# A fused attention and expert kernel: token blocks transposed by VectorE and put in place by transfers, half-height and half-width matmuls for the odd pieces, router and sort at other places

## The chip, the cores and the metric

One Trainium2 chip, one core. The time is device microseconds for one execution. Before the change: median 720.46 us of three runs (720.29 to 722.41). A core has TensorE (PE, matmuls and transposes), VectorE (DVE), ScalarE (ACT), GpSimd (POOL) and SyncE (SP, which here only issues transfers); each runs its own queue in order, and 16 DMA engines move the data.

## What is computed

All in float32. Two layers with a residual each:

- x (16 sequences of 100 tokens, 256 channels) is normalised, projected to queries of 16 heads of 64, and attends to a context of 361 rows of 192 channels (keys and values by projection, softmax, weighted sum). The result is projected back to 256 channels, with a bias, and added to x.
- The sum is normalised again (call it xn). A shared gated network of width 704, `silu(xn w1) * (xn w3)`, then `w2`, is computed for every token. A router of seven experts picks for each token the one of highest probability; that expert, a network of the same form, is computed for the token. Both are added to x with weights that come from the chosen probability.

## The kernel before

The 1600 tokens lie as 13 tiles of 128 (the last, tile 12, has 64 rows) in acc, and in four groups, tiles 0-2, 3-5, 6-8 and 9-12 (GROUPS, L41). xT holds normalised tokens with channels on the partitions, which is what matmuls that contract over channels read: first those of the first normalisation, for the queries, later those of the second, for router and shared network.

**Attention** is a loop over 32 steps s = (sequence b, half g of the heads) (L814), each some 15 us. In a step: scores of four pairs of heads (L645), their exponentials (ACT, L661), 32x32 block transposes on VectorE (L674), matmuls for later sequences put between (key_pairs and value_pairs, both by L568; queries L544), and in g = 0 the weighted sums of the sequence before (values, L717), whose operand aT was put together from the transposed blocks by 16 transfers of 32 partitions each (moved, L681 to L705; eight issued on SP, eight on POOL, L695), with over from row (L701) beside them. The PE order is written out by hand; in attention so are those of ACT, VectorE and SP; the other order follows the program. Scores and the products of L568 contract over 64 rows and run in two halves of the PE array; L717 writes 64 columns each, two side by side.

Small pieces of work are strung between by queues: norms (normalisation and router, one piece by part() behind each VectorE transpose and one at a step's end), turns (the PE transposes of a normalised group, taken at the start of a g = 0 step, L819) and fillers (projection and router, at the end of the scores of a g = 0 step, L856). When the last token of a group has been projected (project, L739), normalised(g, keep=True) strings in its second layer_norm (L166): moments, roots (with a power on POOL, L183), normalise (L188; the result goes to memory xn_d by SP, L197), and turn (L202): two PE transposes a tile by the identity (L208) and one ACT copy for two tiles (L211).

The context of one sequence has 361 = 2 x 128 + 105 rows. For two sequences, the guests (GUESTS, L50), the odd 105 rows travel in the padding of five other sequences' context, the hosts, and their values go by transfer (host, L582) to space in w2_sb.

**Shared network.** hidden (L408) makes for a group the 704 hidden rows: five whole chunks of 128 (L425) and a rest of 64 (HALF, L442), which lies in the upper 64 partitions of a sixth chunk whose lower part is zero. down (L454) contracts the six chunks for each tile (L460), adds the result to acc (L463) and sends it to base_d (SP, L466). Group 0 is done in the last step of attention and behind it, the others behind attention.

**Behind attention** (L936 to L954) the order on PE is: hidden of group 1, transposes of group 3, down of tile 3, router of group 3, down of tiles 4 and 5, the two matmuls of sort_tokens (L314), hidden of group 2, fill (L391, the token of each slot), hidden of group 3, down of groups 2 and 3. Between sort and the rest SP fetches the weights of the first four expert tiles (fetch, L901; 2.2 MB each); behind fill POOL gathers rows of xn_d (L919).

**Experts.** Tokens are sorted by expert in tiles of 128. A Switch (L1032) picks by their number one of seven straight programs of run (L995): eight products for the first part of a tile (L969, 16 matmuls), transposes of the next tile's tokens (turn, L957), three more, and the finish of the tile before (L977, L981), which goes out by POOL. The first turn(0) stands in front of the Switch (L1030).

Of the kernel before, what the change touches and what calls it, by code (L numbers as in the profile page):

```python
# [14 lines left out]
F32 = mybir.dt.float32  # L15
# [11 lines left out]
P = 128  # L27
# [12 lines left out]
HALF = I - NI * P  # L40
GROUPS = ((0, 1, 2), (3, 4, 5), (6, 7, 8), (9, 10, 11, 12))  # L41
FIRST, SECOND = (0, 1), (2, 3, 4, 5)
NS = (N - E) // P + E
NF = (N + P - 1) // P
WE = 2 * 2 * I + (NI + 1) * C
# [1 line left out]


FREE = P - JL
GUESTS = {6: (1, 2, 3, 4, 5), 13: (8, 9, 10, 11, 12)}  # L50
HOSTS = {host: (b, i) for b, hosts in GUESTS.items() for i, host in enumerate(hosts)}
HG = 8
WARM = 6
# [6 lines left out]
def xattn_moe(  # L60
# [66 lines left out]
        nc.tensor.matmul(nothing[:, :P], ones, ones, start=True, stop=True)  # L127

    nc.gpsimd.memset(acc[LAST:, NT - 1, :], 0.0)
    nc.gpsimd.memset(w2_sb[: P - HALF, NI, :], 0.0)  # L130

    def load_x(g):
        full = [t for t in g if t < NT - 1]
# [29 lines left out]

    biases = deque()

    def layer_norm(tiles, keep=False):  # L166


        n = len(tiles)
        of, xns = {}, []  # L170

        def moments(i):
            if i == 0:
                of["mv"] = small.tile([P, 4, 2], F32, name="mv")
                of["rstd"] = small.tile([P, 4], F32, name="rstd")
            st = small.tile([P, 6], F32, name="st")
            nc.vector.bn_stats(st, acc[:, tiles[i], :])
            nc.vector.bn_aggr(of["mv"][:, i, :], st)

        def roots():  # L180
            rstd = of["rstd"]
            nc.vector.tensor_scalar(rstd[:, :n], of["mv"][:, :n, 1], EPS, None, ALU.add)
            nc.gpsimd.tensor_tensor(rstd[:, :n], rstd[:, :n], power[:, :n], ALU.pow)  # L183

        def normalise(i):
            t = tiles[i]
            xn = small.tile([P, C], F32, name="xn", bufs=4)
            nc.vector.tensor_scalar(  # L188
                xn,
                acc[:, t, :],  # L190
                of["mv"][:, i, 0:1],
                of["rstd"][:, i : i + 1],
                ALU.subtract,
                ALU.mult,
            )
            if keep:
                nc.sync.dma_start(xn_d[t * P : t * P + rows(t), :], xn[: rows(t), :])  # L197
            else:
                biases.append(t)
            xns.append(xn)  # L200

        def turn():  # L202
            for i in range(0, n, 2):
                tr = bank()
                m = min(2, n - i)
                for o in range(m):
                    for k in range(2):
                        nc.tensor.transpose(  # L208
                            tr[:, ds((k * m + o) * P, P)], xns[i + o][:, ts(k, P)], ident
                        )  # L210
                nc.scalar.copy(  # L211
                    xT[:, :, ds(tiles[i] * P, m * P)],
                    tr[:, : 2 * m * P].rearrange("p (k n) -> p k n", k=2),
                )

        parts = [lambda i=i: moments(i) for i in range(n)] + [roots]
        return parts + [lambda i=i: normalise(i) for i in range(n)], turn

    def load_shared(i):

        if i < 4:
            k, o = i // 2, ds(i % 2 * I, I)
            nc.sync.dma_start(w13_sb[:, k, o], w13[ts(k, P), o])
        elif i == 4:
            nc.sync.dma_start(w2_sb[:, :3, :], w2[: 3 * P].rearrange("(i p) c -> p i c", p=P))
        else:
            r = w2[3 * P : NI * P].rearrange("(i p) c -> p i c", p=P)
            nc.sync.dma_start(w2_sb[:, 3:NI, :], r)
            nc.sync.dma_start(w2_sb[P - HALF :, NI, :], w2[NI * P :])

    def router(tiles):

# [175 lines left out]
    def hidden(g, hT, sp, width=NB, same_table=0):  # L408
# [1 line left out]

        n = sum(map(rows, g))

        nc.gpsimd.memset(hT[: P - HALF, NI, :n], 0.0)

        def product(to, at):
            for k in range(2):
# [25 lines left out]
        def rest():  # L442

            pa = bank()
            product(pa, NI * P)
            s = sp.tile([P, width], F32, name="s")
            nc.scalar.activation(s[P - HALF :, :n], pa[:HALF, :n], AF.Silu)
            nc.vector.tensor_tensor(
                hT[P - HALF :, NI, :n], pa[P - HALF :, :n], s[P - HALF :, :n], ALU.mult
            )  # L450

        return [lambda i=i: whole(i) for i in range(NI)] + [rest]

    def down(g, hT):  # L454

        for i, t in enumerate(g):
            r = rows(t)
            y = bank()
            for c in range(NI + 1):
                nc.tensor.matmul(  # L460
                    y[:r, :C], hT[:, c, ds(i * P, r)], w2_sb[:, c, :], start=(c == 0), stop=(c == NI)
                )
            nc.vector.scalar_tensor_tensor(  # L463
                acc[:r, t, :], y[:r, :C], coef[:r, t : t + 1], acc[:r, t, :], ALU.mult, ALU.add
            )
            nc.sync.dma_start(base_d[t * P : t * P + r, :], acc[:r, t, :])  # L466


    with ExitStack() as attn:
# [10 lines left out]
        def load_ctx(b, parts=1):  # L480
            cT = ap2.tile([P, NR, NJ * P], F32, name="cT")
            of = ctxT[b].rearrange("p (k n) -> p k n", k=NR)
            for i in range(parts):
                k = ts(i, NR // parts)
                nc.sync.dma_start(cT[:, k], of[:, k])
            return cT

        wq_r = wq.rearrange("p (u k m) -> p u k m", u=NU, k=2)
# [14 lines left out]
        def load_later(s):  # L503

            if 1 < s < 4:
                m = ts(s - 2, NCH // 2)
                nc.sync.dma_start(
                    wp_sb[:, m], wproj.rearrange("(m p) c -> p m c", p=P)[:, m]
                )
            if s == 3:  # L510
                nc.sync.dma_start(rb_sb, rbias.to_broadcast([P, E]))
                nc.sync.dma_start(rw_sb[:, :, :E], rwT.rearrange("(k p) e -> p k e", p=P))
            if s == 4 or s == 7:
                load_x(GROUPS[s // 3 + 1])
            if s == 6 or s == 9:
                normalised(GROUPS[s // 3])
            if 10 <= s < 14:
                load_shared(s - 10)
            if s in (2 * B - 3, 2 * B - 2):
                load_shared(s - 2 * B + 7)  # L520

        NA = 4
        ats, qT_bufs = [], []
# [215 lines left out]
        def project(t):  # L739
            r = rows(t)  # L740
            resT = resTs.pop(t)
            pp = bank()
            for c in range(NCH):
                nc.tensor.matmul(  # L744
                    pp[:r, :C], resT[:, c, QP : QP + r], wp_sb[:, c, :], start=(c == 0), stop=(c == NCH - 1)
# [5 lines left out]
        turns, fillers, norms = deque(), deque(), deque()  # L751

        def normalised(g, keep=False):
            parts, turn = layer_norm(g, keep)
            norms.extend(parts)


# [56 lines left out]
        for s, (b, g) in enumerate(steps):  # L814
# [1 line left out]


            if g == 0:
                while turns:  # L819
                    turns.popleft()()  # L820
                pairs = values_of.pop(b)
                if s == 0:
                    ask = lambda: qs.pop(0)() or (lambda: None)
# [18 lines left out]
            for i in range(n2):  # L842
# [7 lines left out]
                turning = then  # L850
                for _ in range(-(-len(pairs) // (n2 - i))):
                    product(pairs)
            if puts:
                puts.popleft()()
            if g == 0:
# [20 lines left out]
        while norms or fillers or turns:  # L876
# [2 lines left out]
                turns.popleft()()  # L879
            if fillers:  # L880
                fillers.popleft()()
        down(GROUPS[0][:2], hT0)
        for at in range(NG):
            values(B - 1, at, *held.pop(0))
        down(GROUPS[0][2:], hT0[:, :, 2 * P :])
        finished(B - 1)
        while fillers:
            fillers.popleft()()
# [36 lines left out]
            oob_is_err=False,  # L925
        )

    with tc.tile_pool(name="hs", bufs=1) as hs:
        def run_hidden(g):
            n = sum(map(rows, g))  # L930
            hT = hs.tile([P, NI + 1, n], F32, name=f"hT{n}")
            for piece in hidden(g, hT, sp):
                piece()
            return hT

        parts, turn_last = layer_norm(GROUPS[-1], keep=True)  # L936
        for one in parts:
            one()
        hT = run_hidden(GROUPS[1])
        turn_last()  # L940
        down(GROUPS[1][:1], hT)
        for one in router(GROUPS[-1]):
            one()
        down(GROUPS[1][1:], hT[:, :, P:])
        fill = sort_tokens(hs)
        for k in range(NW):
            fetch(k)
        hT2 = run_hidden(GROUPS[2])
        fill()
        for k in range(NX - 1):  # L950
            gather_into(xgs, xn_d, k)
        hT3 = run_hidden(GROUPS[3])
        down(GROUPS[2], hT2)
        down(GROUPS[3], hT3)  # L954
    hp = ctx.enter_context(tc.tile_pool(name="hp", bufs=2))

    def turn(k):  # L957
        tr = bank()
        for j in range(2):
# [1 line left out]
        xgT = xp.tile([P, 2, P], F32, name="xgT")  # L961
        nc.scalar.copy(xgT.rearrange("p k n -> p (k n)"), tr[:, : 2 * P])  # L962
        return xgT

    def products(to, xgT, w, units):

# [10 lines left out]
    def finish(k, hT, bg):  # L977
# [14 lines left out]
            oob_is_err=False,  # L992
        )

    def run(k, state, tiles):  # L995


        xgT, last = state
        w, hT = wexs[k % NW], hTs[k % 2]
        pa, pb, pc = bank(), bank(), bank()  # L1000
        n = (NI - 1) * P
        products(pa, xgT, w, [i * P for i in range(NI - 1)])
        products(pb, xgT, w, [I + HALF + i * P for i in range(NI - 1)])
        s = sp.tile([P, n], F32, name="sg")
        nc.scalar.activation(s, pa[:, :n], AF.Silu)
        nc.vector.tensor_tensor(
# [15 lines left out]
            gather_into(bgs, base_d, k + NX - 1)  # L1022
        if k and k + NW - 1 < tiles:
            fetch(k + NW - 1)
        return ahead, (k, hT, bgs[k % NX])

    n = nc.values_load(e_at[:, NS:], min_val=0, max_val=NS - NF)
    for k in range(NX - 1):
        gather_into(bgs, base_d, k)
    first = turn(0), None  # L1030

    for extra in tc.Switch(n, NS - NF + 1):  # L1032
        then = first
# [57 lines left out]
```

## Time and profile before

| what | value |
|---|---|
| median of the runs | 720.46 us |
| profiled execution, its own time | 722.64 us |
| its span, first to last instruction | 720.9 us |
| VectorE, ScalarE, GpSimd busy | 420.4, 280.5, 198.6 us |
| attention, to the last projection | up to 521.1 us |
| behind attention, to the first expert product | 521.1 to 598.5 us |
| experts, to the last matmul | 598.5 to 715 us |
| DMA engines' mean busy share, those two later stretches | 0.36, 0.68 |

How to read the lines of a profile: a group is line, engine, operation, result and operands with partitions x elements, count, then busy time, the mean length of one in ns, and the idle time ahead of it with what ended it. A line of waits is who waited for whom, microseconds in total, times, the longest. A timeline line is start, length, engine and line. An f32 matmul shows as two passes, so counts of matmuls are doubled; a transpose shows as one. A line of stretches has the stretch, its length, busy time of PE, PEld, VectorE, ScalarE and GpSimd with counts, granted PE clock, share of the DMA engines and GB/s.

### The profile page before, as it was taken

What the parts mean: (1) busy time and instruction counts of PE and PEld (TensorE: products, weight loads), DVE (VectorE), ACT (ScalarE), POOL (GpSimd) and SP (SyncE); (2) the same over time, 40 slices, a digit from 0 to 9 for tenths busy, and PEclk for the clock granted to TensorE, in tenths of its full rate; (3) what the DMA queues carried; (4) which work ended last, traced back from release to release, by engine and by line L of the source; (5) the groups of instructions that cost most, each with busy time, mean ns of one, the idle gap of its engine ahead of it and who ended that gap; (6) DMA issues with size and microseconds to landing.
All of it is one profiled execution on the core that took longest, in us unless ns stands there. A gap on an engine that the chain in (4) does not pass through costs nothing. (4 is left out here: it accounts for less than half of the span.)

```text
span 720.9 us, 14788 instructions
## 1 busy us (share of the span) xinstructions
PE 709.6 (98%) x5192; PEld 511.7 (71%) x5192; DVE 420.4 (58%) x1090; ACT 280.5 (39%) x791; POOL 198.6 (28%) x419
## 2 busy tenths in 40 slices
PE   9999999999999999999999999999999999999996
PEld 6557657667566766757667676656766588999996
DVE  2777866867787676776777768676247222122121
ACT  2564563534546354463644635543032101111110
POOL 4142322322432222422224222242010103343321
PEclk9999999999999999999999999999999999999999
DMA  7066656454484543636445454465004812898860
GB/s 263 21 143 156 163 143 162 93 144 125 115 214 114 155 118 87 169 89 177 103 113 160 111 146 111 115 160 130 30 30 177 355 37 64 313 347 335 309 248 23
DMA packets 54619, 109.38 MB, mean 152 GB/s; under 512 B 28665, under 2 KB 35964, under 8 KB 52612
## 3 DMA queue, kind: packets, MB, share of 16 engines
q1 hardware_dynamic: 43892, 81.94, 37.1%
q0 software_dynamic: 10352, 25.98, 13.7%
q8 instruction: 44, 0.72, 0.4%
q14 instruction: 43, 0.35, 0.2%
q10 hardware_dynamic: 288, 0.39, 0.2%
HBM read 60.96 MB, written 5.35 MB: 92 GB/s over the span
## 5 line engine op out<-in xcount | busy, mean ns | idle before, releaser
L661 ACT ACTIVATE at<-mm,nm 128x361 f32<-128x361 f32 x256 | 141.7, 559 | 171.4 <-DVE nm L658 171.2
L695 POOL DMA_DIRECT2D aT<-tb x256 | 126.1, 500 | 293.2 <-PE mm L717 100.2
L658 DVE TENSOR_REDUCE nm<-mm 128x1 f32<-128x361 f32 x256 | 123.4, 523 | 60.9 <-PE mm L645 60.0
L674 DVE STREAM_TRANSPOSE tb<-at 128x384 f32<-128x384 f32 x256 | 133.0, 558 | 4.5
L568 PE MATMUL mm<-cT,wk_sb 64*128 64x361 f32 x768 | 125.3, 465 | 1.2 <-DMA wk_sb<-in_wk 0.7
L568 PE MATMUL mm<-wv_sb,cT 64*128 64x512 f32 (+1 forms) x552 | 126.1, 589 | 0.0
L568 PEld LDWEIGHTS mm<-cT,wk_sb 64*128 64x128 f32 x768 | 74.8, 187 | 46.6 <-issue 4.2
L645 PE MATMUL mm<-kT,qT 64*128 64x361 f32 x512 | 97.2, 474 | 0.0
L568 PEld LDWEIGHTS mm<-wv_sb,cT 64*128 64x128 f32 (+1 forms) x552 | 53.2, 185 | 53.6 <-issue 43.4
L969 PE MATMUL mm<-xgT,wex 128*128 128x128 f32 x660 | 78.6, 275 | 0.7 <-ACT xgT L962 0.7
L969 PEld LDWEIGHTS mm<-xgT,wex 128*128 128x128 f32 x660 | 77.0, 192 | 1.8 <-issue 1.1
L717 PE MATMUL mm<-aT,v 128*64 128x100 f32 (+1 forms) x1472 | 72.5, 251 | 1.7 <-DMA over<-row 1.3
L645 PEld LDWEIGHTS mm<-kT,qT 64*128 64x128 f32 x512 | 47.7, 186 | 34.2 <-issue 8.8
L717 PEld LDWEIGHTS mm<-aT,v 128*64 128x64 f32 (+1 forms) x1472 | 67.2, 135 | 6.1 <-issue 3.4
L417 PE MATMUL mm<-xT,w_sb 128*128 128x384 f32 (+1 forms) x176 | 60.9, 503 | 0.0
L417 PEld LDWEIGHTS mm<-xT,w_sb 128*128 128x128 f32 x176 | 32.9, 190 | 26.1 <-issue 8.5
L661 ACT ACTIVATION_READ_ACCUMULATOR at<-mm,nm 128x1 f32 x256 | 50.4, 197 | 0.0
L744 PE MATMUL mm<-wp_sb,resT 128*128 128x256 f32 (+1 forms) x208 | 48.0, 384 | 0.0
L544 PE MATMUL mm<-xT,wq_sb 128*128 128x200 f32 x256 | 46.9, 336 | 0.0
L544 PEld LDWEIGHTS mm<-xT,wq_sb 128*128 128x128 f32 x256 | 43.4, 190 | 4.0 <-issue 1.5
L744 PEld LDWEIGHTS mm<-wp_sb,resT 128*128 128x128 f32 (+1 forms) x208 | 37.8, 186 | 11.2 <-issue 4.4
L608 ACT COPY kT<-mm 128x361 f32<-128x361 f32 x64 | 29.3, 460 | 39.5 <-PE mm L568 39.5
(143 smaller groups left out, 561.2 us busy)
## 6 DMA issues: line engine op xcount, KB each, us to landing
wex<-in_wex SPq DMA_DIRECT2D x15, 2176.0 KB
aT<-tb POOLq DMA_DIRECT2D x256, 80.2 KB, 3.1
aT<-tb SPq DMA_DIRECT2D x256, 80.2 KB
cT<-in_ctxT SPq DMA_DIRECT2D x15, 576.0 KB
over<-row SPq DMA_DIRECT2D x64, 100.0 KB
xn_d<-xn SPq DMA_DIRECT2D x12, 128.0 KB
base_d<-acc SPq DMA_DIRECT2D x12, 128.0 KB
w_sb<-in_w SPq DMA_DIRECT2D x4, 352.0 KB
```

Source lines behind the costliest of these rows:

```text
L417: nc.tensor.matmul(to[:, :n], w13_sb[:, k, ds(at, P)], xT[:, k, ds(g[0] * P, n)], start=(k == 0), stop=(k == 1),)
L544: nc.tensor.matmul(pq[:, o, :], wq_sb[:, u, k, ts(o, P)], xT[:, k, ts(g, QG * LQ)], start=(k == 0), stop=(k == 1),)
L568: nc.tensor.matmul(to[o][:height, :width], *operands(o, k), start=(k == 0), stop=(k == NR - 1),)
L608: nc.scalar.copy(kT[:, c, :], to[0][:, :LKV])
L645: nc.tensor.matmul(sc[o][:, :LKV], qTs[b // QG][r, c, ts(b % QG, QB), :], kTs[b][c // 4][r, c % 4, :], start=True, stop=True,)
L658: nc.vector.tensor_reduce(nm[:, o : o + 1], sc[o][:, :LKV], AX.X, ALU.max, negate=True)
L661: nc.scalar.activation(at[:, o, :LKV], sc[o][:, :LKV], AF.Exp, bias=nm[:, o : o + 1], accum_out=sums[:, o : o + 1],)
L674: nc.vector.transpose(tb[:, :, :, o, i * QR : i * QR + 32].rearrange("p j k n -> p k j n"), at[:, o, :].rearrange("p (k j n) -> p k j n", ...
L695: queue.dma_start(aT[ts(j, 32), i].rearrange("p k o n -> p (k o n)"), tb[ts(i, 32), j].rearrange("p k o n -> p (k o n)"),)
L717: nc.tensor.matmul(av[ts(o, DK), i, :], v[:n, ds((2 * c + o) * DK, DK)], aT[:n, :, j, o, ts(i, QR)], start=(j == 0), stop=(j == NJ - 1),)
L744: nc.tensor.matmul(pp[:r, :C], resT[:, c, QP : QP + r], wp_sb[:, c, :], start=(c == 0), stop=(c == NCH - 1))
L969: nc.tensor.matmul(to[:, ts(o, P)], w[:, ds(j * 2 * I + u, P)], xgT[:, j, :], start=(j == 0), stop=(j == 1),)
```

## The change

1. **Blocks.** Second normalisations (keep) are no longer transposed by PE. normalise transposes each tile in 32x32 blocks on VectorE into a scratch (the second half of w13_sb in attention, a tile of its own behind it), and move(k) puts the blocks in place in xT with 16 transfers for each half k of the channels, eight issued on SP and eight on POOL, each 32 partitions by the group's tiles by 32 elements (128 bytes). turn does nothing for them, so ACT's copies go as well. The moves are two more pieces in norms; they fall in steps s = 14, 20 and 28, behind the second or third scores or at the end.
2. **Place of loads.** As the scratch lies in w13_sb, its second half is loaded at s = 28 and w2 at s = 29 (before: at 12 and 13, and 29 and 30). Guest 6 becomes guest 7, its hosts 2 to 6. Context that hosts nobody is loaded without padding. The remaining PE transposes (turns) come behind the first scores and products of a step.
3. **Pairs.** For five pairs of tiles the rests of 64 lie in different halves of the partitions (LOWER), and their last, half-height matmuls follow one another at the end of both tiles' sums. w2's rest is loaded into both halves.
4. **Two halves.** For tile 12, in project and down, the chunks are summed in two halves of 64 columns side by side; ACT copies the second half and VectorE adds both.
5. **Order behind attention.** hidden of group 1, down of 3, 5 and 4, router of group 3, three pieces of hidden of group 2, sort, the rest of group 2, two pieces of group 3, fill and gathers, the rest of group 3, down of 6 and 7, 12, 9 and 10, turn(0), down of 8 and 11, the first 16 products of expert tile 0, then the Switch.

The PE order by the two programs differs, apart from moved turns and guests, in these counts: 52 PE transposes of xn become 26; everything else is split or moved.

```
+PAIRS = ((0, 1), (5, 4), (6, 7), (9, 10), (8, 11))
+LOWER = tuple(b for _, b in PAIRS)
-GUESTS = {6: (1, 2, 3, 4, 5), 13: (8, 9, 10, 11, 12)}
+GUESTS = {7: (2, 3, 4, 5, 6), 13: (8, 9, 10, 11, 12)}
...
             if keep:
                 nc.sync.dma_start(xn_d[t * P : t * P + rows(t), :], xn[: rows(t), :])
+                nc.vector.transpose(xb[:, :, ts(i, 32)], xn.rearrange("p (c n) -> p c n", n=32))
...
+        def move(k):
+            for q in range(4):
+                for c in range(4):
+                    queue = nc.gpsimd if (q + c) % 2 else nc.sync
+                    m = n if q * 32 < LAST else full
+                    to = xT[ts(c, 32), k, ds(tiles[0] * P, m * P)]
+                    of = xb[ts(q, 32), 4 * k + c, : m * 32].rearrange("p (i n) -> p i n", n=32)
+                    queue.dma_start(to.rearrange("p (i n) -> p i n", n=P)[:, :, ts(q, 32)], of)
...
+    def two_halves(y, products):
+        n = len(products) // 2
+        for i in range(n):
+            for o in range(2):
+                nc.tensor.matmul(
+                    y[ts(o, LAST), :C], *products[o * n + i], start=(i == 0), stop=(i == n - 1)
+                )
+        high = bp_sb[:LAST]
+        nc.scalar.copy(high, y[LAST:, :C])
+        return high
...
+        if len(tiles) == 2:
+            for (t, hT, i), y in zip(tiles, ys):
+                r = slice(0, HALF) if t in LOWER else slice(P - HALF, P)
+                nc.tensor.matmul(
+                    y[:, :C], hT[r, NI, ts(i, P)], w2_sb[r, NI, :], start=False, stop=True
+                )
...
+        blocks = hs.tile([P, 8 * P], F32, name="blocks")
+        parts, turn_last = layer_norm(GROUPS[-1], blocks)
+        for one in parts:
+            one()
+        hT = run_hidden(GROUPS[1])
+        down([(3, hT, 0)])
+        down([(5, hT, 2), (4, hT, 1)])
+        for one in router(GROUPS[-1]):
+            one()
+        hT2, pieces = run_hidden(GROUPS[2], 3)
+        fill = sort_tokens(hs)
+        for k in range(NW):
+            fetch(k)
+        for piece in pieces:
+            piece()
+        hT3, pieces = run_hidden(GROUPS[3], 2)
+        fill()
+        for k in range(NX - 1):
+            gather_into(xgs, xn_d, k)
+        for piece in pieces:
+            piece()
+        down([(6, hT2, 0), (7, hT2, 1)])
+        down([(12, hT3, 3)])
+        down([(9, hT3, 0), (10, hT3, 1)])
+        ahead = turn(0)
+        down([(8, hT2, 2), (11, hT3, 2)])
...
-    first = turn(0), None
+    first = ahead, None, first_products(0, ahead)
```

## Prediction

> **What bounds the kernel now.** I read the page first (busy shares and slices), then the waits of TensorE (PE), then PE's timeline around the change, and last the groups of the operations that are added or removed.
>
> ```profile
> PE 709.6 (98%) x5192; PEld 511.7 (71%) x5192; DVE 420.4 (58%) x1090; ACT 280.5 (39%) x791; POOL 198.6 (28%) x419
> PE   9999999999999999999999999999999999999996
> ```
>
> PE is busy in every slice but the last. A busy PE need not be at its peak, so I ask whether it ever waits:
>
> ```profile
> PE mm L717 <- DMA over<-row: 1.3, 1, 1.3
> PE mm L127 <- DVE ones L124: 1.1, 1, 1.1
> PE mm L969 <- ACT xgT L962: 0.7, 1, 0.7
> ```
>
> These are its three longest waits; with the small ones they come to some 6 us of 720.9. So a PE instruction that goes away is worth its own length, anywhere, and any new wait of PE costs its full length. The timeline gives the steps (start, length, group):
>
> ```profile
> 513.97 7.21 PE L744 MATMUL mm<-wp_sb,resT 128*128 128x256 f32 x32
> 521.12 14.46 PE L417 MATMUL mm<-xT,w_sb 128*128 128x384 f32 x44
> 535.41 1.04 PE L208 MATMUL mm<-ident,xn 128*128 128x128 f32 x8
> 536.28 2.76 PE L460 MATMUL mm<-w_sb,hT 128*128 128x256 f32 x12
> 538.97 0.64 PE L240 MATMUL mm<-xT,rw_sb 128*32 128x128 f32 x16
> ...
> 597.33 0.44 PE L960 MATMUL mm<-ident,xg 128*128 128x128 f32 x2
> 598.50 3.81 PE L969 MATMUL mm<-xgT,wex 128*128 128x128 f32 x32 [0.74 <-ACT xgT L962]
> ```
>
> Each f32 matmul is two passes (12 for six matmuls), and a full pass of 256 columns takes 0.22 us. The router's matmuls of the last group (L240) stand 18 us behind the end of the projections (521.12).
>
> **Part 1, PE work removed.** The groups by form:
>
> ```profile
> L568 PE MATMUL mm<-cT,wk_sb 64*128 64x361 f32 x768 | 125.3, 465 | 1.2 <-DMA wk_sb<-in_wk 0.7 <-DMA cT<-in_ctxT 0.5
> L208 PE MATMUL mm<-ident,xn 128*128 128x128 f32 x52 | 7.6, 281 | 0.6 <-DVE xn L188 0.6
> L744 PE MATMUL mm<-wp_sb,resT 128*64 128x256 f32 x16 | 3.7, 382 | 0.0
> L460 PE MATMUL mm<-w_sb,hT 128*64 128x256 f32 x12 | 2.8, 383 | 0.0
> ```
>
> Transposes: 26 of the 52 at L208 go, three sets of 6 in attention (0.78 us each in the timeline) and the 8 at 535.41 (1.04): 3.4 us.
>
> Last tile in two halves: L568 shows what two half arrays side by side bring: 163 ns a pass (125.3/768) where 361 columns on the full array would be 361 x 0.857 = 309 (14.46/44/384 = 0.857 ns a column). The 16 passes of L744 then take about 8.5 steps of 0.22 and the 12 of L460 about 6.5: 1.9 and 1.4 us in place of 3.7 and 2.8, less 0.1 each for the change of mode: 3.0 saved, say 2.9. The 64-column pairs of L717 do worse (67 ns against 86 for 100 columns); by that ratio it would be 1.4. I take 2.9, since 256 columns are longer than a weight load of 64 columns (137 ns), which 100 are not.
>
> Pairs: in five pairs two full chunks (4 passes, 0.88 us) become two half-height ones. Alone, the second pass of the first runs beside the first of the second: three steps, 0.66 us. Here a rule speaks against the change: the Trainium skill (TensorEngine Tiling (Array Packing), Tiling Modes, Key Properties) says that a change of tiling mode drains TensorE. The timeline agrees: a score pair (L645) right behind the column-split L717 takes 0.71 us from start to start, one between half-height products 0.61, so some 0.1. Without the drain five pairs save 1.1 us; with one drain each (the way back I count as hidden) 0.6; with two, nothing. I take 0.7, range 0 to 1.8.
>
> Idle: turn(0) moves in front of the last pair (4.4 us and more of PE), which hides the 0.74 us wait: 0.7. Sum removed: 3.4 + 2.9 + 0.7 + 0.7 = 7.7 us.
>
> **Part 2, what is added on PE.** The branch (Switch) now stands behind 16 products of the first expert tile and in front of its other six. Before, it lay in the gap from 597.33 to 598.50. So it costs 0 (PE's queue covers it) to 1.1; I take 0.5. ScalarE, VectorE and the DMA queues branch earlier than they need.
>
> **Part 3, the blocks in attention (groups 0 to 2).** Per group: three VectorE transposes of 128x256, 0.39 us each as an estimate (L674: 558 ns for 384 columns); ScalarE loses two copies of 0.6; 32 DMAs, 16 on SP and 16 on POOL, of 128-byte runs, 96 or 128 runs each. VectorE is 58% busy and PE waits for it nowhere; I cost these at nothing. The DMAs stand in steps with g = 0, behind the moved() of the step before and in front of their own step's. SP needs about 16 x 0.6 = 10 us (the two issues of over at 307.52, with 256 runs each, took 1.30 together). What queues behind is row, aT and over of that step, which PE reads two steps (some 30 us) later. POOL has the same place and 8 aT (4 us) behind it: 16 x t + 4 us in 30. Free up to t = 1.6 us an issue, and the router reads these blocks two steps later. The late loads of w13 (s = 28) wait for the moves on SP and have two steps before their first reader. The shift of the guest by one batch changes no count of matmuls. Cost 0; if cover failed, each of three groups would stop PE at L717.
>
> **Part 4, the blocks in front of the experts.** Here the cover is thin. After the change the projections end 2.3 + 0.1 + 1.7 earlier, T = 517.0. The normalisation chain took 5.8 us before (521.12 to 526.90). It grows by a ScalarE copy and a second add (0.75) and four transposes (1.6): moves can start at T + 8.1 = 525.1. PE reaches the router after hidden (14.3 us from start to start) and the three downs (16 chunks at 0.44 and a pair, 7.8): T + 22.1 = 539.1. So 14.0 us are there for 16 issues on POOL and the landing of the last:
>
> ```profile
> L695 POOL DMA_DIRECT2D aT<-tb x256 | 126.1, 500 | 293.2 <-PE mm L717 100.2 <-PE mm L208 41.1 <-DVE nm L658 39.7
> L919 POOL DMA_INDIRECT xg<-xn_d,slot_token x15 | 15.2, 1015 | 25.3 <-DMA wex<-in_wex 17.7 <-PE mm L969 2.5 <-DMA aT<-tb 2.2
> ```
>
> A POOL issue with 32 runs takes 0.50 us, an indirect one with 128 rows 1.0. Landing is 3.1 us in the median (DMA issues of the page). The new one is direct like the first and has as many runs as the second. With t = 0.5: 8.0 + 3.1 = 11.1, no wait. With t = 1.0: 19.1, a wait of 5.1. I take t = 0.8: 15.9, a wait of 1.9. The rule against it: the Trainium skill (DMA: Bandwidth & Descriptors, Anatomy of one DMA) fits a POOL-issued DMA as 2.0 us plus bytes/436e3. 16 KB one after another would be 16 x 2.04 = 33 us, a wait of 19 to 22. But eight aT issues of 80 KB each pass in 3.9 us here, so fixed parts overlap, and the row goes before the fit. The DMA engines themselves:
>
> ```profile
> 308.00:311.00 3.00, 3.00 (x18) 1.39 (x16) 2.32 (x6) 2.02 (x6) 0.00 (x0) 1.00 0.49 108
> ```
>
> In this stretch mostly the 512 runs of over move: 0.49 x 3 us x 16 engines / 512 = 46 ns a run at most. 3584 runs on 16 engines are 10.3 us, within the 14. SP issues (10 us) land in time too.
>
> Behind the router: its VectorE chain took 5.7 us (538.97 to 544.7) and now has 7.9 (three pieces of hidden). Sort to fill: 9 us of VectorE (545.5 to 554.5) against some 13 of PE. The four expert weights had landed at 573.7 (DMA shares in stretches of 2 us), 29 us behind the sort's matmuls; now some 43 pass until first_products. The gathers have 22 us before turn(0). All at nothing.
>
> **Sum.** -7.7 + 0.5 + 1.9 = -5.3 us: the span goes from 720.9 to 715.6. The profiled execution took 722.64, 2.2 more than the median 720.46 and 1.7 more than its span; the same difference from the median gives 715.2.
>
> **Rivals.** (A) The cover holds, t at or below 0.65: -7.2 and the pairs between 0.7 and their best, 711.9 to 713.9, middle 713. For it: POOL's aT issues hardly vary. (B) The likeliest, t of 0.65 to 1.05: a wait of 0 to 6, 713.9 to 718.3. (C) Half arrays don't overlap when they stand alone (ratio of L717, pairs nothing: removed 5.5) and the wait is 4 or more: 719.5, within the noise. For it: L717's ratio; against: L568's. (D) Slower: POOL's issue of strided short runs. Break-even is 16t + 3.1 - 14.0 = 7.2, t = 1.13 us. At the skill's 2.04 the wait is 21.7 and the time 720.46 - 7.2 + 21.7 = 735, and beyond t = 1.6 the aT transfers in attention would be late as well. For it: no run of before shows 96 or 128 short runs from POOL; against: both rows above are below 1.13.
>
> **Numbers.** A 0.33, B 0.38, C 0.17, D 0.12. Range 711.8 to 720.2, which leaves D and the ends out. 0.3% (2.2 us) is about what a measurement of this kernel can tell from no change: faster (below 718.3) 0.72, same 0.16, slower 0.12.
>
> **What would show it.** Right: L208 at 26 passes; PE busy lower by about 7 us; a PE wait at L240 for a DMA xT, 0 to 5 us, as the only new one; POOL's xT issues at 0.6 to 1.0 us. Wrong: PE waits at L717 for aT or over in steps with moves, xT issues above 1.1 us, a gap of over 1 us behind the 16 first products, or the half passes at L460 and L744 at 0.2 us each.

## The result and the profile after

The median of seven runs is 727.13 us (724.04 to 729.97), beside 720.71 us for the kernel before (seven runs, 720.29 to 722.75): 1.0079 times as long, with a 95% interval of 1.0061 to 1.0096. The forecast was 715.2, faster; it is slower. The profiled execution took 725.76 us with a span of 723.9.

The page of the changed kernel, busy times and slices (a digit is a tenth of the slice):

```profile
PE 707.0 (98%) x5166; PEld 511.1 (71%) x5166; DVE 425.6 (59%) x1113; ACT 276.9 (38%) x785; POOL 232.0 (32%) x481
PE   9999999999998999999999999989999998999996
```

26 matmul records fewer, as foreseen, but PE's busy time fell by only 2.6 us where 7.0 were expected, and three slices are no longer full. Idle time (span less busy) rose from 11.3 to 16.9 us. The longest waits of TensorE in the changed kernel (sum, times, longest):

```profile
PE mm L781 <- DMA over<-row: 3.1, 1, 3.1
PE mm L709 <- ACT at L725: 2.7, 1, 2.7
PE mm L1001 <- DVE hgT L1091: 2.0, 1, 2.0
```

The second and third have no like in the list of before. The first has (L717 there, 1.3 us), but at another place, 204.86 in the timeline of before. The one new wait that was forecast, the router's (L265 here, L240 before), is not there. Each of the three happens once; PE's timeline (start, length, group, and in brackets the idle time just before) places them:

```profile
224.30 0.88 PE L709 MATMUL mm<-kT,qT 64*128 64x361 f32 x4
227.84 1.89 PE L709 MATMUL mm<-kT,qT 64*128 64x361 f32 x8 [2.65 <-ACT at L725]
...
481.18 3.38 PE L781 MATMUL mm<-aT,v 128*64 128x100 f32 x48 [3.12 <-DMA over<-row]
...
603.73 0.41 PE L1001 MATMUL mm<-ident,xg 128*128 128x128 f32 x2 [1.98 <-DVE hgT L1091]
603.97 6.71 PE L1048 MATMUL mm<-xgT,wex 128*128 128x128 f32 x44
```

I call them W1 (attention step s = 14), W2 (the weighted sums at the end of s = 30) and W3 (behind the 16 products that now stand in front of the Switch). The name of a releaser is inferred, and W2's is misleading: L781 reads aT and v, while over is read by VectorE (L796). In e2 below the same wait is put down to aT, and in e4 PE goes on at 474.84, only 0.4 us after the last issue of over had ended. So I read W2 as a wait for the aT that SP issues just ahead of over.

The lengths hold a second loss. The 44 passes at 603.97 take 6.71 us; before, the same 44 took 5.08:

```profile
602.37 5.08 PE L969 MATMUL mm<-xgT,wex 128*128 128x128 f32 x44
```

The stretches of after (length, PE busy, granted clock, DMA share, GB/s) say why, here those behind W1:

```profile
228.00:230.00 2.00, 2.00 (x9) 0.91 0.82 195
230.00:232.00 2.00, 2.00 (x6) 0.50 0.86 254
232.00:234.00 2.00, 2.00 (x8) 0.74 0.65 187
```

Read each row's clock as a mixture of 1.0 and 0.5: 0.36 + 2.0 + 1.04 = 3.4 us at half the clock, which costs 1.7 us of work. The same happens behind W2 (482.2 to 485.6) and W3 (605.1 to 608.5). The kernel before shows no such drop until its last 5 us.

This gives an account of the profiled execution. PE's work went down by 7.8 us (709.6 to 701.8, the busy time of the kernel e12 below, which does the changed work without a drop), the three drops add 5.2 (the rest of the busy time, 707.0 less 701.8; three times the 1.7 read from the clock would be 5.1), idle time adds 5.6: 3.0 in all, from 720.9 to 723.9. The medians lie further apart (6.4 us), since the profiled execution of before was 1.9 above its median (722.64) and that of after 1.4 below. The other executions of after have mean clocks of 0.986 (729.97 us) to 0.993 (724.04 us), those of before mostly 0.998 to 0.999. A drop of 3.4 us lowers the mean by 3.4 x 0.5 / 724 = 0.0023, so that by this estimate they hold two to five each; the profiled one held three. Five is more than W1 to W3 account for, and where the others fall no trace shows.

### The profile page after: what moved, and what is told of

Same layout as the page of the kernel before. It is cut to its first block, busy times and chain, and to the rows that moved or that the text cites. A ratio compares the mean times of both kernels' runs of the same rounds, so it can differ in the third digit from the quotient of the medians.

```text
span 723.9 us, 14995 instructions
## 1 busy us (share of the span) xinstructions
PE 707.0 (98%) x5166; PEld 511.1 (71%) x5166; DVE 425.6 (59%) x1113; ACT 276.9 (38%) x785; POOL 232.0 (32%) x481
## 5 line engine op out<-in xcount | busy, mean ns | idle before, releaser
L1048 PEld LDWEIGHTS mm<-xgT,wex 128*128 128x128 f32 x660 | 78.6, 195 | 1.0 <-issue 0.3
L781 PE MATMUL mm<-aT,v 128*64 128x100 f32 (+1 forms) x1472 | 73.6, 253 | 3.5 <-DMA over<-row 3.1
L781 PEld LDWEIGHTS mm<-aT,v 128*64 128x64 f32 (+1 forms) x1472 | 68.1, 136 | 8.0 <-ACT pr L291 3.3
L813 PE MATMUL mm<-wp_sb,resT 128*128 128x256 f32 x192 | 46.1, 395 | 0.0
L813 PEld LDWEIGHTS mm<-wp_sb,resT 128*128 128x128 f32 x192 | 36.9, 196 | 10.1 <-issue 2.5
```

The lines of the kernel that those rows point to most:

```text
L781: nc.tensor.matmul(av[ts(o, DK), i, :], v[:n, ds((2 * c + o) * DK, DK)], aT[:n, :, j, o, ts(i, QR)], start=(j == 0), stop=(j == NJ - 1),)
L813: nc.tensor.matmul(pp[:r, :C], resT[:, c, QP : QP + r], wp_sb[:, c, :], start=(c == 0), stop=(c == NCH - 1))
L1048: nc.tensor.matmul(to[:, ts(o, P)], w[:, ds(j * 2 * I + u, P)], xgT[:, j, :], start=(j == 0), stop=(j == 1),)
```

## The experiments

The theory behind the first four: three separate places, each with its own cause (the turns' new place, the loads of the shared weights behind the moves on SP, the products in front of the Switch), each a wait and a drop of the clock. The rival: the blocks' transfers disturb attention in general, or the drops come from PE's load as a whole, so that undoing one place moves the loss elsewhere. All ran in three rounds. Ratios are to the kernel before on the same chip.

| kernel | median us (range) | ratio [95%] |
|---|---|---|
| e1: after, Switch first | 723.75 (720.83 to 726.46) | 1.0038 [1.0021, 1.0056] |
| e2: after, turns first | 722.31 (720.14 to 724.74) | 1.0031 [1.0014, 1.0048] |
| e3: after, loads at s = 29 | 720.70 (718.50 to 722.34) | 0.9995 [0.9982, 1.0008] |
| e4: all three | 714.94 (714.92 to 716.02) | 0.9927 [0.9910, 0.9943] |
| e5: before, products ahead of the Switch | 722.74 (721.61 to 725.31) | 1.0027 [1.0016, 1.0038] |
| e6: before, turns behind the first products | 724.73 (723.78 to 725.26) | 1.0049 [1.0032, 1.0065] |
| e7: after, W1 filled | 724.58 (721.79 to 727.14) | 1.0063 [1.0038, 1.0087] |
| e8: after again | 726.39 (724.54 to 728.40) | 1.0085 [1.0065, 1.0105] |
| e9: e4 without blocks | 716.83 (715.97 to 717.98) | 0.9949 [0.9932, 0.9966] |
| e10: e4 without pairs | 716.14 (714.35 to 716.78) | 0.9930 [0.9913, 0.9946] |
| e11: e9 with the loads at s = 28 | 716.46 (716.23 to 716.66) | 0.9943 [0.9926, 0.9959] |
| e12: e4 again | 715.33 (715.09 to 716.87) | 0.9934 [0.9917, 0.9950] |

**e1, the Switch before the products.**

```
-    first = ahead, None, first_products(0, ahead)
+    first = ahead, None, None
```

> The changed kernel, with the 16 first products of expert tile 0 behind the Switch again; turn(0) stays where the change put it. Theory (each of three new TensorE waits costs its own length and then some 1.7 us of halved clock; the third, 1.98 us at 603.7, is the Switch standing between products and transposes): the wait and the clock drop at 604 to 608 go, 3.7 us below the changed kernel, about 723.4 in the median; the other two waits stay. Rival 1 (the halved clock comes from denser TensorE work and not from waits): the wait goes, 2 us, and the drop comes at another place, 725.1. Rival 2 (the wait is for a PSUM bank that VectorE frees, as the trace labels it): nothing changes, 727.

3.4 us less than after. W3 and its drop are gone; what stands there is a shorter wait for the bank of the last down. PE's timeline of e1:

```profile
600.06 3.81 PE L1048 MATMUL mm<-xgT,wex 128*128 128x128 f32 x32 [1.22 <-DVE acc L525]
```

W1 (2.65) and W2 (4.03) stay, each with its drop.

**e2, the turns at the start of the step, as before.**

```
             if g == 0:
+                while turns:
+                    turns.popleft()()
...
-                while g == i == 0 and turns:
-                    turns.popleft()()
```

> The changed kernel, with the remaining TensorE transposes at the start of a g = 0 step again. Theory (VectorE's normalise of group 0 has no free xn buffer until the transposes of group 3 have run; behind the first scores and products they run one product later, so VectorE stands 3.3 us and TensorE runs out of PSUM banks): the wait of 2.65 us at 227.8 and its clock drop go, 4.3 us below the changed kernel, about 722.8. Rival (VectorE is late by the three added block transposes of 0.45 us in that step): the wait stays at 1.5 us or more, gain below 2 us.

4.8 us less. W1 is gone without a remainder, although the block transposes that the rival blames are still there; W2 (3.43, with a drop) and W3 (1.71, without) stay.

**e3, the second half of w13 loaded one step later.**

```
-            if s in (2 * B - 4, 2 * B - 3):
-                for i in range(2):
-                    load_shared(2 * (s - 2 * B + 5) + i)
+            if s == 2 * B - 3:
+                for i in range(2, 6):
+                    load_shared(i)
```

> The changed kernel, with the second half of w13 loaded at s = 29 behind that step's transfers and not at s = 28. Theory (at s = 28 SP issues 16 moves in 11.4 us and then the two loads, so row, aT and over of s = 29 leave some 3 us later): over of s = 29 leaves about 2.5 us earlier, the wait of 3.1 us at L781 falls to about 1 and brings no clock drop, 4 us below the changed kernel, about 723. Rival (the moves alone make SP late; the loads of 0.9 us are nothing): the wait falls by 1 us to about 2.2, with a clock drop still, 726.

6.4 us less, more than W2 and its drop explain. W2 shrinks to 0.40 us ahead of the sums and 0.88 in their middle, and brings no drop; but in the profiled execution W1 (2.65) brought none either, and W3 (1.91) did. How many drops an execution takes varies, and that W2's absence lowers their number elsewhere is not shown.

**e4, all three.**

> All three edits together (first products behind the Switch, transposes at the start of the step, w13 at s = 29). Theory: the costs add, 3.7 + 4.3 + 4 = 12 us below the changed kernel: span about 712, median 713 to 715, clock 0.998 or more, no TensorE wait above 1.5 us. Rival (the waits hide one another, or another wait takes their place): above 718.

714.94, 5.8 us faster than before and 12.2 below after's 727.13. The single gains, against the same 727.13 (3.4, 4.8, 6.4), sum to 14.6; against e8, after's second measurement, each is 0.7 less, and they sum to 12.4 against 11.5. Page and waits of e4:

```profile
PE 701.3 (98%) x5166; PEld 506.6 (71%) x5166; DVE 425.2 (60%) x1113; ACT 277.4 (39%) x785; POOL 232.1 (33%) x481
```

```profile
PE mm L632 <- DMA cT<-in_ctxT: 1.3, 2, 0.7
PE mm L132 <- DVE ones L129: 1.1, 1, 1.1
PE mm L781 <- DMA aT<-tb: 1.1, 1, 1.1
PE mm L1048 <- DVE acc L525: 1.0, 1, 1.0
```

No wait above 1.1 us, no drop of the clock before the last 5 us, and PE's work is 8.3 us below that of before. The rival falls: undone together, the three places leave little behind. What stays of W2 is the third line (the moves are still there), of W3 the fourth (a bank of the last down, as in e1).

**e5 and e6, one part alone on the kernel before.** e5 takes the 16 products out of run and puts them in front of the Switch; e6 takes the turns behind the first scores and products.

```
...
-    first = turn(0), None
+    ahead = turn(0)
+    first = ahead, None, first_products(0, ahead)
```

> The kernel before, with one part alone: the 16 first products of expert tile 0 in front of the Switch. Theory (the Switch takes TensorE's sequencer some 2 us, hidden before in the wait for xgT and in the queue ahead of it): a wait of some 2 us in front of the second transposes and a clock drop behind it, 3.7 above before, 724.4. Rival (the wait in the changed kernel comes from its own bank order): no wait, 720.7.

```
             if g == 0:
-                while turns:
-                    turns.popleft()()
...
+                while g == i == 0 and turns:
+                    turns.popleft()()
```

> The kernel before, with one part alone: TensorE transposes behind the first scores and products of a step (guests, blocks and loads as before). Theory a (place of the transposes alone): VectorE stands some 3 us in step 14, TensorE waits 2 us or more with a clock drop, 724.5 or more. Theory b (it needs the guest's missing value product as well: here step 14 has one product more to run meanwhile): wait below 1 us, no drop, within 1 us of 720.7.

PE's timeline of e5, where only the Switch's place is changed:

```profile
603.73 0.41 PE L960 MATMUL mm<-ident,xg 128*128 128x128 f32 x2 [2.20 <-issue]
```

The gap is the Switch's own: PE waited for nothing the profile shows ("issue"), and the VectorE operation named at W3 in after had ended 0.7 us before PE went on (1.4 in e5), so it was only the last thing to have happened. Here the gap brought no drop in the profiled execution, and the price is 1.8 us, not the 3.7 of a gap with one. PE's timeline of e6:

```profile
229.68 3.08 PE L645 MATMUL mm<-kT,qT 64*128 64x361 f32 x8 [1.75 <-ACT at L661]
```

The turns' place alone makes the wait, without a block or a move in the kernel (the clock is 0.50 from 232 to 234), and costs 3.8 us. For the mechanism, VectorE's timeline, of before, of e6 and of after:

```profile
223.55 0.41 DVE L188 TENSOR_SCALAR xn<-acc,mv,rstd 128x256 f32<-128x256 f32 x1 [0.93 <-PE mm L208]
```

```profile
226.58 0.41 DVE L188 TENSOR_SCALAR xn<-acc,mv,rstd 128x256 f32<-128x256 f32 x1 [4.11 <-PE mm L208]
```

```profile
223.83 0.41 DVE L197 TENSOR_SCALAR xn<-acc,mv,rstd 128x256 f32<-128x256 f32 x1 [3.27 <-PE mm L229]
```

VectorE's next normalise (of another group, in this step too) needs one of four xn buffers, all held by the tiles that the turns have still to transpose. In e6 the turns stand one scores and one product, some 3 us, further back on PE, and VectorE, which runs in order, stands 4.11 us in place of 0.93. In after it stands 3.27 us; the clock times of before and after are alike because, with the guest moved, this step begins one product earlier in after. Behind VectorE wait the row maxima, ScalarE's exponentials for those (in after 6.14 us at 227.13), and PE for the banks that these free. More xn buffers would test the same link; this was not tried.

**e7 and e8, W1 filled with work.** e7 is after, with six matmuls of a projection of values done a second time into the same banks behind the second scores of s = 14; e8 is after unchanged, beside it.

```
...
+                    def repeat():
+                        for k in range(NR):
+                            for o in range(2):
+                                nc.tensor.matmul(
+                                    to[o][:n, :512], *operands(o, k), start=(k == 0), stop=(k == NR - 1)
+                                )
...
+                if i == 1 and again:
+                    again.pop()()
```

> The changed kernel, and in step 14 behind the second scores the 6 value matmuls (2.7 us) once more, into the same banks with the same result: TensorE works where it would wait at 227.8. Theory (idleness, not what is waited for, sets off the halved clock): no wait above 1 us there, no clock drop at 228 to 234; the filler takes as long as the wait, so 1.7 us below the changed kernel. Rival (the drop answers to load or to time): the drop at 228 to 234 stays, time as the changed kernel or up to 0.5 above.

> The changed kernel itself, as the yardstick of this call. Theory: again three TensorE waits of 2 us and more, 724 to 730 us, the more the lower the mean clock, some 2 us for 0.0024 of it. Rival (the first measurement was one chip's): near 720.

In e7's timeline of PE the fill takes the place of the wait, and the clock from 228 to 234 is 1.00:

```profile
225.65 2.74 PE L698 MATMUL mm<-wv_sb,cT 64*128 64x512 f32 x12
228.47 2.38 PE L719 MATMUL mm<-kT,qT 64*128 64x361 f32 x8
```

12 added passes make the kernel no slower: the median is 1.8 us below e8's, about one drop, but the ranges overlap, so the times leave the question open. One trace cannot settle it either: in this execution W2 (3.66) and W3 (1.79) brought no drop, and in e3 W1 brought none unfilled. A wait allows a drop and doesn't force it. That drops follow gaps rests on all the traces together (under "The clock" below), not on e7. e8 repeats after: its gaps of 2.65 and 3.16 us brought a drop each, that of 1.73 none.

**e9 to e12, which gains are real.** e9 is e4 with PE's transposes in place of all blocks and moves, e11 is e9 with the loads at s = 28, e10 is e4 without pairs, e12 is e4 again.

```
-                nc.vector.transpose(xb[:, :, ts(i, 32)], xn.rearrange("p (c n) -> p c n", n=32))
...
-            if keep:
-                return
...
-        if keep:
-            parts += [lambda k=k: move(k) for k in range(2)]
...
+        turn_last()
```

> All three edits, and TensorE transposes in the place of all blocks and moves (halves, pairs, order and loads kept). Theory (the blocks are worth the TensorE time of 26 transposes, 3.4 us, and cost nothing where no queue is late): 3.4 above the kernel with all three edits, 718.3. Rival (moves cost as much elsewhere as they save): within 1 us of it.

```
-LOWER = tuple(b for _, b in PAIRS)
-SINGLE = tuple(t for t in range(NT) if not any(t in p for p in PAIRS))
+LOWER = ()
+SINGLE = tuple(range(NT))
...
```

> All three edits, without the pairs: the rest of 64 is again a full sixth chunk for every tile. Theory (a pair takes 0.66 to 0.70 us where two full chunks take 0.88): 5 x 0.2 = 1.0 us above the kernel with all three edits, 716. Rival (two half heights run fully side by side): 2 us above, 717.

```
-            if s == 2 * B - 3:
-                for i in range(2, 6):
-                    load_shared(i)
+            if s in (2 * B - 4, 2 * B - 3):
+                for i in range(2):
+                    load_shared(2 * (s - 2 * B + 5) + i)
```

> As the one without blocks, but with w13's second half loaded at s = 28 as in the changed kernel. Theory (the wait for over came from SP being full: 16 moves of 11.4 us and the loads together; loads alone find SP idle): no wait above 1.5 us at L781, within 1 us of the one without blocks. Rival (the loads' own bytes or place make the wait): a wait of 2 us or more there, 2 to 4 us above.

> The kernel with all three edits once more, as the yardstick of this call: 714.9 to 716.0, no clock drop before the end.

Blocks: e9 has 3.3 us more of PE work than e12 (705.1 against 701.8), as priced, but is only 1.5 slower by the medians, with ranges that overlap. In e12 the sums at the end of s = 30 still wait 0.49 + 0.92 us, in e9 0.34; the rest of the difference lies in small waits that vary. Pairs: 0.8 us by the medians, inside their scatter, and 1.8 by PE's busy time (703.6 against 701.8), which differs by 0.5 between e4 and e12, the same kernel. Loads: e11 is not slower than e9, and no wait in it is above 1.2 us. SP has no moves there and stands idle for 6.3 us behind the loads of s = 28. So the whole of W2 needs moves and early loads together; the moves alone leave about 1 us of it (e3, e4, e12).

## Why the prediction was wrong, point by point

Three terms failed: the cost 0 for the blocks in attention (Part 3), the 0.5 for the Switch (Part 2), and the turns, which had no term at all. That a wait also brings down the clock was priced nowhere. The terms are the prediction's; the last column is the profiled execution of after, unless another kernel is named.

| step | forecast us | measured us |
|---|---|---|
| PE transposes | -3.4 | -3.3 (e9 against e12) |
| two halves | -2.9 | -3.1 |
| pairs | -0.7 | -1.2 in the timeline, -0.8 in e10 against e12 |
| wait at turn(0) | -0.7 | -0.7 |
| Switch behind products | +0.5 | +2.0, and a drop |
| blocks in attention, loads | 0 | +3.1 (W2), and a drop |
| turns' new place | none | +2.65 (W1), and a drop |
| router's wait | +1.9 | 0 |
| drops of the clock | none | +5.2 |

The lines sum to 4.7 us and the span grew by 3.0; most of the difference is in small waits that come and go between executions (in before 1.3 us at 204.86 and 1.2 in the first 50 us, in after 0.8 more for context).

In sum, PE's work was right (7.8 measured, 7.0 forecast). Idle time was forecast at +1.7 and came out at +5.6, and the drops were not forecast at all: 3.9 + 5.2 - 0.8 = 8.3 us, the distance from 715.6 to the span's 723.9.

**Part 1 held.** Two rows of PE's timeline in after show it:

```profile
522.39 1.95 PE L495 MATMUL mm<-wp_sb,resT 128*64 128x256 f32 x16
...
545.57 0.70 PE L519 MATMUL mm<-w_sb,hT 64*128 64x256 f32 x4
546.20 0.64 PE L265 MATMUL mm<-xT,rw_sb 128*32 128x128 f32 x16
```

16 half passes take 1.95 us (1.9 forecast), and 12 take 1.5 (1.4). A pair's four records take 0.63 us to the next start, one change of mode included, in place of 0.88: nearer the price without a drain (0.66) than with two. Rival C is out. A sum among the rivals was off: for B, waits of 0 to 6 us on top of 720.46 - 7.2 are 713.3 to 719.3 us, not 713.9 to 718.3.

**Part 4 was wrong in its size.** The router starts at 546.20 with no wait. POOL's timeline of after, with the 16 issues:

```profile
531.26 2.79 POOL L219 DMA_DIRECT2D xT<-blocks  x5 [2.84 <-DVE blocks L207]
534.82 5.95 POOL L219 DMA_DIRECT2D xT<-blocks  x11 [0.77 <-issue]
```

An issue took 0.55 us, not 0.8: near the direct row with 32 runs (0.50), not the indirect one, and landed in 1.7 us in the median, not 3.1. The last was out at 540.8 (on SP at 542.0), 5.4 us before the router. That is rival A's t, and rival D's slow issue did not occur. The slower side came from elsewhere.

**Part 3 is the step that failed in its cover.** It said that what queues behind the moves on SP is read two steps later. That is true of the step that has the moves, s = 28. But SP is in order, so the delay goes on to the transfers of s = 29, whose aT PE reads one step later. PE's timeline of before at this place shows what slack there was, and e3's what the moves leave without the loads:

```profile
475.28 4.78 PE L717 MATMUL mm<-aT,v 128*64 128x100 f32 x96 [0.34 <-DMA aT<-tb]
```

```profile
478.01 2.35 PE L781 MATMUL mm<-aT,v 128*64 128x100 f32 x48 [0.88 <-DMA aT<-tb]
```

SP's timeline, first of before, then of after:

```profile
468.32 5.01 SPq L695 DMA_DIRECT2D aT<-tb  x8
473.37 1.90 SPq L701 DMA_DIRECT2D over<-row  x2
```

```profile
450.86 11.38 SPq L219 DMA_DIRECT2D xT<-w_sb  x16
...
468.39 1.31 SPq L765 DMA_DIRECT2D over<-row  x2
470.02 0.86 SPq L247 DMA_DIRECT2D w_sb<-in_w  x2
...
471.66 6.79 SPq L759 DMA_DIRECT2D aT<-tb  x8
478.49 1.31 SPq L765 DMA_DIRECT2D over<-row  x2
```

The moves hold SP until 462.2 (11.4 us, where the prediction had 10), the over of s = 28 is out only at 469.7, then the loads. The last aT of s = 29 is out at 478.45 instead of 473.33 (start and length of the eight), while PE reaches these sums within 0.5 us of when it did before. There was little slack: PE waited 0.34 us for an aT at this place before the change already. Two parts of the delay come together. With the loads in front the eight aT issues took 6.0 to 7.5 us (after, e1, e2, e7, e8), without them 5.0 to 5.9 (e3, e4, e12), and the wait in the middle of the sums fell to 0.88 us in e3; why the loads lengthen the issues no run shows. Without the moves (e11) the one wait left was 0.34. Before's 1.3 us wait that opened the prediction lay at 204.86, another step, so it is no measure of the slack here.

**The turns (a line in the change list) were not priced.** The prediction counted the PE transposes that go and treated the ones that stay as the same work elsewhere. It did not ask what they release: xn buffers, for which VectorE waits (e6). That VectorE "is 58% busy and PE waits for it nowhere" was not quite so even in before (1.1 us at L127 and 0.6 at L208, both in lines that the prediction shows), and it could hold only for that order.

**The Switch was priced between 0 and 1.1 us,** from the idle time around it before; it is 2.0 us in W3 and 2.2 in e5, and 1.7 to 1.9 in the traces of e2, e3, e7 and e8. A gap of over 1 us behind the 16 products was one of the prediction's own signs of being wrong. Before, a part was hidden under other waits, as in e1 and e4, where the gap in front of the first products is 1.0 to 1.2 us and ends with a bank coming free. The Trainium skill (Runtime: NRT & Kernel Launch, Instruction fetch mechanics) says that a taken branch to outside the fetched window stalls on the fetch. It gives no figure for such a stall, and no run here separates the fetch from the branch itself, so what the Switch does in these 2 us stays open.

**The clock.** That a wait could cost more than its length was in no step. The Trainium skill (TensorE: Matmul & The Clock Gate, HAM oscillation — how this bites in real kernels) puts the abstract rule as "no PE-idle gaps >~3.4µs". By it W1, W2 and W3 (2.65, 3.12, 1.98) would cost their length, 7.75 us as an estimate; with the measured drops they cost 12.95. The measurement decides: of the 16 gaps of 1.7 us or more in the profiled executions of these kernels, ten were followed by 3.4 us at half clock, and none of the shorter ones was. The six traces without such a gap (before, e4, e9 to e12) have no drop before the last 5 us. What else decides whether a gap brings one is open.

## What to carry to other kernels

When PE is busy 98% of the time and the work taken away is sure, price the waits of everything that is moved: follow an in-order queue until it has caught up, not only through the step in which it is loaded, and ask of each moved instruction which buffers it frees and who is waiting for them. A new TensorE gap of about 2 us should be priced at its length and, about as likely as not, 1.7 us more (here three of seven gaps of 1.7 to 2.2 us brought a drop, and seven of nine longer ones). Undoing the three placements and keeping the work that was saved (e4) brought nearly exactly the forecast time, 714.94 and 715.33 in its two measurements. That this fits so well is in part luck: PE's work fell by 7.8 to 8.3 us instead of 7.0, the router's wait did not come, and the span of e4 is 713.2 us where 715.6 was forecast.

## What the runs showed of the hardware

- Gaps of 1.71 to 4.03 us on TensorE were followed by a drop of the clock to 0.50 for 3.4 us in ten of 16 cases, gaps up to 1.36 us in none. The drop began 2.7 to 4.5 us after the gap did, sometimes with PE at work again for 1.8 us. The same gap may bring it in one execution and not in the next (W1 with 2.65 us: yes in after, e1, e8, no in e3). The times spread with it: 724.04 us at a mean clock of 0.993 to 729.97 at 0.986 in after, but 714.92 to 716.02 in e4.
- A GpSimd issue of a transfer with 96 or 128 runs of 128 bytes took 0.55 us, one with 32 runs 0.50; the number of runs hardly counts. On SyncE the first kind took 0.60 us in the median, but up to 1.99, so that 16 of them held the queue for 10.3 to 13.3 us.
- A Switch with matmuls right in front of it left TensorE idle for 1.7 to 2.2 us (six traces).
